# Transposed blocks of the attention probabilities: one store to DRAM and four loads for each four heads, in place of 16 copies from SBUF to SBUF

## The chip, the cores and the metric

The kernel runs on one core of a Trainium2 chip, in one launch. The metric is the device time in microseconds (us). Three runs of the kernel before gave 1243.25, 1243.53 and 1244.83 us; their median, 1243.53 us, is the time to compare with. The profile comes from an execution of its own, which took 1242.96 us.

## What is computed

The reference is one block of a transformer with a mixture of experts, all of it in float32: 16 sequences of 256 tokens with 256 channels, 16 heads of 64, and 8 experts with 1024 hidden channels. Cut to what matters here:

```python
shift = silu(t) @ W_ada.T + b_ada
h = ln(x) + shift
q, k, v = heads(h @ Wqkv.T)            # q and k are normalised per head
attn = softmax(q @ k.T / sqrt(64))     # 256 x 256 for each head and sequence
x = x + merge(attn @ v) @ Wout.T
tok = x.reshape(-1, 256)               # 4096 tokens
gate = softmax(tok @ Wgate.T)
vals, idx = top_k(gate.T, 512)         # each expert takes its best 512 tokens
tok[idx] += gelu(ln(tok[idx]) @ fc1.T + b1) @ fc2.T * vals
```

The product `attn @ v` sums over the keys, so TensorE wants the probabilities with the keys on the partitions, while the softmax leaves the queries there. The change is in how the probabilities are turned round.

## The kernel before, in words

**The stages.** For each sequence b (16 of them) the kernel normalises the tokens (`First`), projects them in twelve groups of 512 columns (`Group`: queries, keys and values for each half of the tokens), works through the attention in four steps of four heads (`Quad`, d = 0 to 3), and closes with the output projection, the residual and the gate logits for each of the two halves of the tokens (`Tail`). When the gates of the first 15 sequences are known, a search of 30 steps over the bits of the gate values (`Routing`) finds each expert's threshold. Each step is a comparison on VectorE, a count on TensorE (tile `pc`) and a decision on VectorE, and each needs the one before it. The experts (`Job`) follow, and the last sequence is routed beside them.

**One Quad.** `scores` puts the scores of two heads into PSUM (L612), `maxima` takes the row maxima on VectorE (L619), `exps` the exponentials on ScalarE (L628), `normalise` divides on GpSimd (L639). `turn` (L649) transposes on VectorE within blocks of 32 x 32, from `pr` into `pb`: it leaves each block on its own 32 partitions, so that the blocks still have to change partitions. `shuffle` (L661) does this: for each of four groups of 32 source partitions (k) and each of four groups of 32 target partitions (q) it issues one copy of 64 KB on SyncE's queue, from `pb` to `prT`, both in SBUF. `product` (L672) then multiplies `prT` by the values into `po` on TensorE, and `evict` (L683) copies `po` out on ScalarE. `pb` and `prT` have two buffers each, 8 KB in each partition, and `po` has one.

**The order.** Nothing runs in the order of the source. Every step is recorded with `at(place, engine, duration, function, needs, makes, tiles, lag)`; `Plan.order` plays all steps through with these durations, always takes on a free engine the ready step with the smallest place, and emits the instructions in the order that results. The tables `PLACES` (one list for the first, the second, the inner and the last two sequences) and `OTHERS` hold the places. So the durations and lags given there, and the tables, decide in which order each engine's queue holds its instructions; on the chip each engine works through its queue in order and waits at each instruction for what it needs. The steps in question, with the durations that the plan takes for them:

```python
at(p + 13, "SP", 6.8, a.shuffle, [pb], [prT], [pb, prT], lag=2.4)
at(p + 22 + i, "PE", 0.87, partial(a.product, i), [prT, ("v", b, g)], [po], [po, prT, ("v", b)], mode=2, lag=0.25)
```

SyncE's queue (SP) also carries the loads of the inputs `xs` (L396), the stores of the tokens `out` (L705) and of the normalised tokens `xn_dram` (L715), and, from the routing on, the loads of the experts' weights (L965 to L969). The instruction that waits there holds up all that stand behind it.

Of the kernel before, what the change touches and what calls it, by code (L numbers as in the profile page):

```python
# [9 lines left out]
F32 = mybir.dt.float32  # L10
# [8 lines left out]
P = 128  # L19
B, N, D = 16, 256, 256  # L20
# [6 lines left out]
TB = N // P  # L27
# [7 lines left out]
SQ = 32  # L35
QB = P // SQ
GW = 512
# [105 lines left out]
def kernel(  # L143
# [14 lines left out]
    nc = tc.nc  # L158
# [68 lines left out]
    def make_others():  # L227
# [32 lines left out]
            -1072.21, -115.42, -267.12, -318.46, -283.78, -263.97, -343.54, -141.99, -236.37,  # L260
            -14.78, -117.8, -186.09, -160.29, 25.3, -57.16, -43.18, -123.28, -79.21, -42.36,
            -113.65, 19.5, -72.88, -20, -70.8, -105.24, 11.94, -75.55, 182.09, -53.2, 2.24,
            -32.28, -39.46, 109.35, 45.26, -50.6, 154.41, -26.02, -58.37, -126.26, -142.08,
            210.89, -27.08, -38.07, -37.13, 5.73, 56.69, -23.35, -19.55, -25.71, -35.68, -18.12,
            74.55, 7.69, -21.8, 114.43, 8.66, -10.45, 70.24, 156.18, 1.21, 12.27, 1.88, 131.08,
            -15.51, 119.21, 116.23, -1.79, 79.85, -8.01, -63.9, -48.12, -63.85, -73.53, 47.46,
            -99.13, -127.82, -186.87, -153.57, 84.76, -127.47, -28.96, 127.88, -174.52, -111.4,
            -104.14, -19.09, -47.87, -8.05, 80.09, -63.95, 106.51, -63.42, -122.29, -8.5,
            171.03, -189.33, -37.82, 290.18, 281.18, -29.55, 19.38, 112, 128.87, -12.2, 186.07,
            91.29, 46.71, 173.2, 114.86, -9.77, 109.32, 149.87, -2.6, -9.22, 0.91, -13.41,  # L270
            134.45, 44.98, -24.62, -65.96, -17.99, -3.34, 260.18, -7.67, 17.8, 35.74, 230.8,
            -2.03, 167.88, 59.79, 281.61, 33.31, 279.56, 29.61, 22.41, 106.55, 15.76, 44.1,
            17.21, 11.13, 77.2, 165.28, 142.54, -60.91, -3.37, 69.59, 88, 16.75, 337.51, 91.2,
            34.07, 4.36, 19.11, 45.9, 31.58, 8.25, 114.95, 164.25, 23.63, 54.39, 128.79, 117.81,
            29.1, 147.8, 161.75, 207.73, 239.85, -42.55, 34.67, 125.98, 63.81, 65.48, 87.98,
            -22.22, 40.48, 79.92, 130.41, 49.27, 238.8, 60.37, 155.11, 191.23, 86.22, 164.95,
            161.39, 80.09, 90.21, 56.48, 51.85,
        ),
        1: (
            -1032.77, 129.62, -236.19, -178.16, -149.32, -47.96, -192.61, -79.27, 33.09, -10.98,  # L280
            -69.57, 52.12, -62.93, 196.91, -51.34, 58.21, 154.36, -36.67, -14.18, 55.12, -44.86,
            61.84, -27.82, -5.29, -36.21, 126.18, 82.92, -42.83, -28.04, 101.38, -11.56, -33.27,
            115.69, 59.37, -41.86, -34.28, 36.18, 48, -29.52, -1.38, 130.85, 23.18, -26.62,
            21.73, 23.95, -26.66, 22.46, -16.79, 104.79, -25.2, 16.34, 21.7, -17.15, -14.75,
            120.88, -18.87, 64.57, -12.33, -22.41, 12.98, -13.56, 129.3, 86.67, -10.79, -0.15,
            -14.51, 18.77, -4.63, 129.64, 13.06, -38.88, -1.19, 53.22, 95.23, 2.6, -15.23,
            55.21, 14.48, 121.02, -6.64, 96.51, 53.51, -5.52, 38.03, -5.28, 133.71, -4.22,
            291.78, 38.02, 1.66, 144.11, 3.99, 31.85, -2.69, 183, -82.98, -23.55, 44.17, 57.53,
            13.82, 7.93, 121.24, 28.25, 7.73, 230.34, 24.33, 57.51, 56.5, 185.27, 15.11, 155.8,
            8.4, 18.56, 19.91, 14, 69.92, 48.81, 184.98, -14.57, -46.18, 61.75, 40.25, 119,  # L290
            0.56, 294.7, 12.02, 16.1, 4.67, 93.62, 16.4, 231.42, 36.38, 76.89, 89.11, 17.69,
            119.85, 148.17, 157.6, 18.58, 64.15, 136.41, 119.23, 93.08, 1.87, 2.62, 24.02,
            181.34, 32.12, 294.16, 72.21, 85.72, 23.9, 318.14, 148.32, 111.52, 7.8, 159.92,
            81.55, 33.83, 42.79, 146.1, 106.8, 29.25, 189.76, 83.08, 261.31, 125.98, 19.94,
            222.2, 133.41, 47.61, 112.18, 196.94, 88.54, 185.36, 217.24, 77.64, 74.55, 155.64,
            63.8, 252.59, 208.61, 85.49, 155.93, 79.33, 114.81, 72.16, 81.95, 89.11,
        ),
        7: (
            -136.6, 28.37, -210.72, -195.86, 106.16, 217.69, -207.27, 16.33, -60.67, 77.55,
            -55.88, -39.27, -51.01, 63.44, -48.12, -45.3, -11.11, -53.32, -35.85, -45.42, 11.39,  # L300
            -42.14, -24.52, 104.14, -46.62, 127.86, -16.95, -39.73, -42.11, 44.56, -17.26,
            -44.54, 36.77, 24.84, -38.59, 83.06, -21.91, -43.85, 219.41, -45.58, 199.34, 56.38,
            -36.69, -22.93, 5.22, -11.48, -23, 64.04, -34.53, -36.25, 113.75, -22.27, 214.83,
            -17.15, -6.77, -16.98, -18.81, -18.51, 151.77, -14.04, -8.89, -3.49, 10.95, -14,
            32.32, -14.28, 20.86, -8.78, -0.9, 87.46, -11.05, -2.93, 5.15, -10.42, 52.71, -5.41,
            57.43, 12.4, 23.37, -11.7, 35.64, 43.51, 53.16, 136.74, 101.97, 69.01, -1.54,
            246.65, 13.35, 2.69, 125.8, 2.34, 17.7, 44.42, -8.16, -27.24, 35.18, 158.76, 154.51,
            6.05, 68.56, 90.55, 211.51, 6.57, 87.13, 145.2, 18.76, 60.22, 125.88, 11.56, 135.85,
            15.4, 132.04, 67.4, 12.06, 86.81, 113.28, 44.43, 112.93, -19.04, -6.2, 145.87,
            31.58, 15.43, 161.05, 94.62, 131.83, 14.43, 71.38, 119.46, 290, 39.56, 151.25,  # L310
            93.87, 19.72, 169.02, 127.15, 45.38, 20.48, 41.14, 61.17, 183.17, 80.13, -3.1,
            27.05, 17.75, 56.16, 20.46, 277.99, 206.07, 104.18, 22.24, 70.57, 154.95, 146.92,
            37.98, 34.46, 87.02, 31.68, 60.48, 90.07, 47.36, 26.9, 69.95, 217.97, 57.1, 299.85,
            12.13, 146.35, 63.74, 80.61, 163.92, 222.82, 99.04, 73.18, 334, 64.46, 129.48, 71.3,
            79.93, 277.53, 173.17, 111.17, 330.87, 101.91, 94.77, 82.32, 120.45, 87.81,
        ),
        14: (
            -148.14, -203, -234.48, -237.91, 55.19, 13.44, -208.2, 38.61, -85.25, 81.97, -56.75,
            -17.65, -54.82, -22.75, -43.34, 107.24, 56.31, -60.46, -60.46, -44.39, -5.57,
            -50.76, 57.85, -38.65, -34.07, -34.22, -28.53, 50.07, -28.8, 77.55, 65.27, -54.99,  # L320
            -24.28, -45.45, -41.95, 43.06, -39.78, 16.46, 82.74, -2.8, 243.5, 82.1, -30.81,
            58.24, -10.38, -27.02, -21.75, 54.73, 33.7, -29.06, -22.77, 185.55, 94.16, -22.99,
            237.62, -22.46, -28.6, -6.64, -6.52, -19.5, 47.39, -23.44, 189.71, -16.88, -12.68,
            24.5, 108.76, -14.16, -13.79, 22.95, -21.66, -27.51, 66.22, 100.67, -7.05, -23.3,
            -14.3, 94.87, -21.87, -12.56, 54.22, -22.99, 32.84, -3.13, 166.41, -12.6, -8.66,
            88.05, 83.14, -3.53, 87.02, -4.59, -11.23, 4.89, 61.68, -27.92, 65.35, 62.04, 83.34,
            2.36, 3.96, 173.51, 117.22, 5.12, -5.35, 59.99, 48.05, 74.16, 137.59, 200.97, 5.88,
            3.1, 109.29, 79.47, 7.14, 115.94, 9.24, 28.59, -1.22, -1.02, 64.19, 129.58, 136.77,
            12.87, 38.68, 215.83, 16.25, 16.68, 36.84, 15.14, 170.59, 89.28, 284.22, 95.61,
            16.71, 214.12, 191.35, 94.06, 26.68, 16.76, 202.03, 240.43, 145.78, 10.7, 11.64,  # L330
            45.82, 171.36, 30.75, 305.13, 43.03, 105.79, 28.98, 188.53, 165.45, 141.02, 27.29,
            47.93, 222.73, 34.77, 86.81, 131.92, 66.48, 31.53, 46.64, 55.06, 94.94, 292.48,
            12.99, 127.48, 63.84, 87.84, 48.33, 196.73, 81.43, 120, 476.87, 68.18, 57.54,
            141.33, 68.28, 126.03, 174.39, 148.26, 318.47, 55.44, 239.95, 72.76, 135.74, 72.97,
        ),
        15: (
            -96.34, 57.5, -135.71, -164.35, 65.69, -163.41, -140.57, 25.18, -76.44, -14.76,
            -67.45, 31.26, -64.27, 60.26, -64.64, -55.24, -7.71, -56.48, -52.05, -39.56, -59.56,
            10.57, -38.4, 101.96, -46.67, 127.7, -41.61, -47.88, -29.51, -0.69, -10.21, -51.73,
# [42 lines left out]
    if True:  # L382
# [216 lines left out]
        class Quad:  # L599
# [44 lines left out]
            def turn(self, i, j):  # L644


                if self.pb is None:
                    self.pb = work.tile([P, 2 * QB, 4, TB, SQ], F32, tag="pb", bufs=2, name="pb")
# [442 lines left out]
        at = plan.step  # L1091
# [276 lines left out]
```

## Time and profile before

| what | value |
|---|---|
| median of three runs | 1243.53 us |
| the profiled execution | 1242.96 us |
| its span on the core | 1241.2 us |
| TensorE matmuls busy | 1092.9 us, 88% |
| VectorE busy | 805.5 us, 65% |
| ScalarE busy | 591.2 us, 48% |
| GpSimd busy | 576.4 us, 46% |
| moved by DMA | 129.54 MB, 104 GB/s on the mean |
| of it read from HBM and written to it | 48.56 MB and 12.58 MB |
| `shuffle` copies | 1024 of 64 KB |

The span is what lies between the first and the last instruction of the core; 1.8 us of the execution lie outside it. In the profile, PE is TensorE's matmul side and PEld its weight loads; DVE is VectorE, ACT is ScalarE, POOL is GpSimd and SP is SyncE (SPq in the rows of its DMA issues). A row "out<-in" names the tile that an instruction writes and the tiles that it reads, without buffer numbers. "Idle before" is the time that an engine stood still ahead of the instructions of a row, followed by what ended the wait.

By the rows of SyncE, the stores of `xn_dram` that begin each later sequence's tail stand at 262.67 us and, eight sequences on, at 698.35 us. The attention stage runs from about 31 to 907 us, the search from 907.06 to 960.74 us, and the experts from 985.45 us to the end.

### The profile page before, as it was taken

How to read it: one execution, taken by the hardware profiler on the slowest of the kernel's cores; microseconds unless marked ns; L12 is line 12 of the kernel's file. 1: busy time of each engine (PE TensorE's matmuls, PEld its weight loads, DVE VectorE, ACT ScalarE, POOL GpSimd, SP SyncE). 2: the span in 40 equal slices, each digit the busy share in tenths (PEclk: the TensorE clock that was granted, in tenths of full speed). 3: DMA queues.
4: the chain of work that ended last, by engine and by line, in shares of the span. 5: the costliest groups of instructions: out<-in, count | busy, mean ns of one | idle time of the engine just before them, and what ended most of it. 6: DMA issues, size and time to landing. Idle time of an engine off the chain costs nothing. (4 is left out here: it accounts for less than half of the span.)

```text
span 1241.2 us, 18995 instructions
## 1 busy us (share of the span) xinstructions
PE 1092.9 (88%) x5787; PEld 721.4 (58%) x5787; DVE 805.5 (65%) x2364; ACT 591.2 (48%) x1661; POOL 576.4 (46%) x805
## 2 busy tenths in 40 slices
PE   6888899899999989999998999989933699999996
PEld 4444555465555646555564656546511588888886
DVE  6657566667776666776767677757656648855540
ACT  1556455556555556655546555555510333333331
POOL 2556445546555554565555455545430233333332
PEclk9899999999999999999999999999956799999999
DMA  5023233333334233332423333323521345656661
GB/s 188 1 68 81 73 91 96 93 92 93 95 81 108 78 102 97 94 99 69 113 74 101 93 92 85 105 73 102 151 76 35 107 146 171 192 162 187 190 187 33
DMA packets 128661, 129.54 MB, mean 104 GB/s; under 512 B 20272, under 2 KB 121904, under 8 KB 128560
## 3 DMA queue, kind: packets, MB, share of 16 engines
q1 hardware_dynamic: 118784, 116.20, 32.8%
q0 software_dynamic: 6144, 8.39, 3.6%
q10 hardware_dynamic: 3632, 3.74, 0.9%
q8 instruction: 47, 0.77, 0.3%
q14 instruction: 54, 0.44, 0.1%
HBM read 48.56 MB, written 12.58 MB: 49 GB/s over the span
## 5 line engine op out<-in xcount | busy, mean ns | idle before, releaser
L537 PE MATMUL pm<-wq,hT 128*128 128x512 f32 x768 | 357.6, 605 | 7.7 <-issue 4.9
L181 POOL TENSOR_TENSOR ss<-ss,neghalf 128x8 f32<-128x8 f32 x128 | 210.9, 1651 | 271.2 <-DVE ss L558 268.4
L639 POOL TENSOR_SCALAR pr<-pr,sums 128x256 f32<-128x256 f32 x512 | 235.9, 478 | 79.5 <-DVE sums L635 79.5
L628 ACT ACTIVATE pr<-sc,nmax 128x256 f32<-128x256 f32 x512 | 237.7, 479 | 30.7 <-DVE nmax L619 24.8
L537 PEld LDWEIGHTS pm<-wq,hT 128*128 128x128 f32 x768 | 139.1, 193 | 152.2 <-issue 138.8
L672 PE MATMUL po<-prT,v 128*64 128x256 f32 x1024 | 136.5, 406 | 84.8 <-DMA prT<-pb 71.6
L619 DVE TENSOR_REDUCE nmax<-sc 128x2 f32<-128x512 f32 x256 | 164.7, 674 | 53.9 <-PE sc L612 53.7
L649 DVE STREAM_TRANSPOSE pb<-pr 128x512 f32<-128x512 f32 x256 | 175.3, 698 | 31.8 <-POOL pr L639 18.5
L672 PEld LDWEIGHTS po<-prT,v 128*64 128x64 f32 x1024 | 78.9, 142 | 142.3 <-issue 79.3
L612 PE MATMUL sc<-kT,qT 64*128 64x256 f32 x1024 | 146.8, 407 | 0.8 <-DVE ss L558 0.6
L612 PEld LDWEIGHTS sc<-kT,qT 64*128 64x128 f32 x1024 | 90.8, 189 | 57.9 <-issue 46.1
L554 DVE TENSOR_REDUCE ss<-sq 128x8 f32<-128x512 f32 x128 | 86.5, 676 | 56.9 <-ACT sq L550 56.3
L683 ACT COPY oT<-po 128x512 f32<-128x512 f32 x64 | 37.5, 585 | 176.7 <-PE po L672 176.7
L1047 PE MATMUL ph<-xT,w 128*128 128x256 f32 x512 | 119.7, 388 | 0.1
L694 PE MATMUL pw<-wo,oT 128*128 128x256 f32 x512 | 116.7, 381 | 0.0
L1063 PE MATMUL py<-w,hid 128*128 128x256 f32 x512 | 116.3, 380 | 0.0
L570 DVE TENSOR_TENSOR qk<-pm,ss 128x512 f32<-128x512 f32 x128 | 86.5, 683 | 34.1 <-POOL ss L181 33.2
L628 ACT ACTIVATION_READ_ACCUMULATOR pr<-sc,nmax 128x1 f32 x512 | 108.3, 212 | 0.0
L694 PEld LDWEIGHTS pw<-wo,oT 128*128 128x128 f32 x512 | 96.2, 191 | 19.3 <-issue 7.0
L1080 POOL DMA_INDIRECT out<-y,idx x32 | 51.4, 1605 | 120.7 <-DVE y L1074 71.3
L1047 PEld LDWEIGHTS ph<-xT,w 128*128 128x128 f32 x512 | 96.9, 193 | 13.6 <-ACT xT L1035 0.2
L1063 PEld LDWEIGHTS py<-w,hid 128*128 128x128 f32 x512 | 95.6, 190 | 12.8
(133 smaller groups left out, 1078.6 us busy)
## 6 DMA issues: line engine op xcount, KB each, us to landing
prT<-pb SPq DMA_DIRECT2D x1024, 64.0 KB, 2.0
w<-in_fc2T SPq DMA_DIRECT2D x16, 1024.0 KB, 5.5
w<-in_fc1T SPq DMA_DIRECT2D x16, 1024.0 KB, 8.0
xn_dram<-tn SPq DMA_DIRECT2D x32, 128.0 KB, 1.8
out<-tok SPq DMA_DIRECT2D x32, 128.0 KB, 2.0
xs<-in_x SPq DMA_DIRECT2D x12, 256.0 KB, 3.0
b<-in_b2s SPq DMA_DIRECT2D x16, 128.0 KB, 8.1
wq<-in_wqkvT SPq DMA_DIRECT2D x3, 512.0 KB, 6.1
```

Source lines behind the costliest of these rows:

```text
L181: nc.gpsimd.tensor_tensor(dst, src, neghalf[:, : src.shape[1]], ALU.pow)
L537: nc.tensor.matmul(self.pm, hTs[self.b][:, c, bass.ts(self.t, P)], wq[:, c, bass.ts(self.g, GW)], start=(c == 0), stop=(c == DC - 1),)
L554: nc.vector.tensor_reduce(self.ss[:, 0, :], self.sq.rearrange("p (h d) -> p h d", d=HD), AX.X, ALU.add,)
L612: nc.tensor.matmul(self.sc[i, j][:, t, :], qTs[self.b][rows, hp, bass.ts(t, P)], kTs[self.b][rows, hp, :], start=True, stop=True,)
L619: nc.vector.tensor_reduce(self.nmax[i, j], self.sc[i, j], AX.X, ALU.max, negate=True)
L628: nc.scalar.activation(self.pr[i, j][:, t, :], self.sc[i, j][:, t, :], AF.Exp, bias=self.nmax[i, j][:, t : t + 1], scale=1.0, accum_out=se ...
L639: nc.gpsimd.tensor_scalar(self.pr[i, j][:, t, :], self.pr[i, j][:, t, :], self.sums[i][:, 1, j, t : t + 1], 1.0, ALU.mult, ALU.mult,)
L649: nc.vector.transpose(self.pb[:, :, 2 * i + j].rearrange("p k t n -> p t k n"), self.pr[i, j].rearrange("p t (k m) -> p t k m", m=SQ),)
L672: nc.tensor.matmul(self.po[j * HD : (j + 1) * HD, i, :], vs[self.b][:, c, bass.ts(4 * self.d + 2 * i + j, HD)], self.prT[:, c, :, 2 * i + ...
L694: nc.tensor.matmul(self.pw, oTs[self.b][:, hp // 2, self.t, hp % 2, :], wo[:, hp, :], start=(hp == 0), stop=(hp == HP - 1),)
L1047: nc.tensor.matmul(self.ph[f], self.w1[:, c, bass.ts(f, P)], self.xT[:, c, :], start=(c == 0), stop=(c == DC - 1),)
L1063: nc.tensor.matmul(self.py[i], self.hid[:, f, bass.ts(i, P)], self.w2[:, f, :], start=(f == 0), stop=(f == FC - 1),)
```

## The change

`turn` writes `pb` in another order of blocks, `shuffle` goes, and two steps take its place. `away` stores the whole of `pb` (1 MB, 8 KB from each of the 128 partitions) to a DRAM tile `blocks`, and `back` reads it in four loads of 256 KB, each into 32 partitions, in runs of 2 KB. `product` reads `prT` with its dimensions in the new order. `blocks` has two buffers. In the plan the one step on SP of 6.8 us with a lag of 2.4 becomes one of 0.4 us with a lag of 5.0 and one of 1.8 us with a lag of 4.0; the lag after each TensorE step goes from 0.25 to 0.22; and the tables `PLACES` and `OTHERS` hold other numbers throughout, so that the order on every engine is another one. The core of the diff:

```diff
                 if self.pb is None:
-                    self.pb = work.tile([P, 2 * QB, 4, TB, SQ], F32, tag="pb", bufs=2, name="pb")
+                    self.pb = work.tile([P, QB, TB, 4, TB, SQ], F32, tag="pb", bufs=2, name="pb")
                 nc.vector.transpose(
-                    self.pb[:, :, 2 * i + j].rearrange("p k t n -> p t k n"),
-                    self.pr[i, j].rearrange("p t (k m) -> p t k m", m=SQ),
-                )
-
-            def shuffle(self):
-                self.prT = work.tile([P, TB, QB, 4, TB * SQ], F32, tag="prT", bufs=2, name="prT")
-                src = self.pb.rearrange("p (c k) h t n -> p c k (h t n)", c=TB)
-                for k in range(QB):
-                    for q in range(QB):
-                        nc.sync.dma_start(
-                            self.prT[bass.ts(q, SQ), :, k].rearrange("p c h n -> p c (h n)"),
-                            src[bass.ts(k, SQ), :, q],
-                        )
+                    self.pb[:, :, :, 2 * i + j].rearrange("p k c t n -> p t c k n"),
+                    self.pr[i, j].rearrange("p t (c k m) -> p t c k m", c=TB, m=SQ),
+                )
+
+            def away(self):
+                self.blocks = dram.tile([QB, SQ, QB, GW], F32, tag="blocks", bufs=2, name="blocks")
+                nc.sync.dma_start(
+                    self.blocks.rearrange("k m q n -> (k m) (q n)"),
+                    self.pb.rearrange("p q c h t n -> p (q c h t n)"),
+                )
+
+            def back(self):
+                self.prT = work.tile([P, QB, TB, 4, TB * SQ], F32, tag="prT", bufs=2, name="prT")
+                for q in range(QB):
+                    nc.sync.dma_start(
+                        self.prT[bass.ts(q, SQ)].rearrange("p k c h n -> p k (c h n)"),
+                        self.blocks[:, :, q].rearrange("k m n -> m k n"),
+                    )
...
-                            self.prT[:, c, :, 2 * i + j, :],
+                            self.prT[:, :, c, 2 * i + j, :],
...
-            sums=4, pr=5, pb=2, prT=2, tok=3, tn=2, tokT=2, pa=1, l1=4, l2=4,
+            sums=4, pr=5, pb=2, prT=2, blocks=2, tok=3, tn=2, tokT=2, pa=1, l1=4, l2=4,
...
-                    at(p + 22 + i, "PE", 0.87, partial(a.product, i), [prT, ("v", b, g)], [po], [po, prT, ("v", b)], mode=2, lag=0.25)
-                at(p + 13, "SP", 6.8, a.shuffle, [pb], [prT], [pb, prT], lag=2.4)
+                    at(p + 22 + i, "PE", 0.87, partial(a.product, i), [prT, ("v", b, g)], [po], [po, prT, ("v", b)], mode=2, lag=0.22)
+                blocks = ("blocks",) + n
+                at(p + 13, "SP", 0.4, a.away, [pb], [blocks], [pb, blocks], lag=5.0)
+                at(p + 18, "SP", 1.8, a.back, [blocks], [prT], [blocks, prT], lag=4.0)
```

## The prediction

> **What bounds the kernel now.** First the page: busy shares and slices.
>
> ```profile
> PE 1092.9 (88%) x5787; PEld 721.4 (58%) x5787; DVE 805.5 (65%) x2364; ACT 591.2 (48%) x1661; POOL 576.4 (46%) x805
> ...
> PE   6888899899999989999998999989933699999996
> ...
> PEclk9899999999999999999999999999956799999999
> DMA  5023233333334233332423333323521345656661
> ```
>
> TensorE is nearly full in the attention (slices 2 to 28) and in the experts (the last ten); between them lies the search, with PE at 3. The DMA engines are a third busy in the attention, so they don't bind by bandwidth. Next, the groups and the list of waits, for what ends TensorE's idle time:
>
> ```profile
> L672 PE MATMUL po<-prT,v 128*64 128x256 f32 x1024 | 136.5, 406 | 84.8 <-DMA prT<-pb 71.6
> ...
> L649 DVE STREAM_TRANSPOSE pb<-pr 128x512 f32<-128x512 f32 x256 | 175.3, 698 | 31.8 <-POOL pr L639 18.5
> ```
> ```profile
> PE po L672 <- DMA prT<-pb: 71.6, 41, 10.5
> PE pc L868 <- DVE reach L859: 22.8, 26, 1.1
> PE pls L1003 <- DVE gates L737: 8.3, 1, 8.3
> PE pm L537 <- issue: 4.9, 1, 4.9
> ```
>
> Ahead of `product` TensorE stood still for 84.8 us, mostly for the copies of `shuffle`; hardly anything else in the attention holds it. By stage, the idle time put before L672 (waits list with windows, all releasers) is 20.9 us up to 262 us, 32.7 in the eight sequences from 262 to 698, 16.0 from 698 to 908 and 15.4 in the search. Last, one of these waits in order of time, on SP's queue and on PE:
>
> ```profile
> 534.01 10.19 SPq L661 DMA_DIRECT2D prT<-pb  x16
> 544.30 0.53 SPq L396 DMA_DIRECT2D xs<-in_x  x1
> ```
> ```profile
> 543.23 1.88 PE L537 MATMUL pm<-wq,hT 128*128 128x512 f32 x4
> 546.12 1.95 PE L672 MATMUL po<-prT,v 128*64 128x256 f32 x16 [1.01 <-DMA prT<-pb]
> ```
>
> The 16 copies take 10.19 us to issue (0.64 each), the last lands 2.0 us after its issue, and `product` starts 12.1 us after the first. The bound is not bandwidth but one queue's rate of issue. The plan reckoned with 6.8 + 2.4 = 9.2 us, so it placed `product` some 3 us too early. Four times a sequence that makes 32.7 / 8 = 4.1 us; the period is (698.35 - 262.67) / 8 = 54.5 us, so TensorE has 50.4 us of work in each.
>
> **What the change costs, part by part.** Durations come from these DMA rows:
>
> ```profile
> prT<-pb SPq DMA_DIRECT2D x1024, 64.0 KB, 2.0
> w<-in_fc2T SPq DMA_DIRECT2D x16, 1024.0 KB, 5.5
> w<-in_fc1T SPq DMA_DIRECT2D x16, 1024.0 KB, 8.0
> xn_dram<-tn SPq DMA_DIRECT2D x32, 128.0 KB, 1.8
> out<-tok SPq DMA_DIRECT2D x32, 128.0 KB, 2.0
> xs<-in_x SPq DMA_DIRECT2D x12, 256.0 KB, 3.0
> ```
>
> *Removed:* 16 issues x 0.64 = 10.2 us of SP for each Quad.
>
> *The store (`away`).* No row shows 1 MB stored. It lies between the 128 KB stores (1.8 us) and `fc1T`, 1 MB queued behind another (8.0); I take 5.5, the row of its size. With 0.1 us for the wait ahead, 5.6.
>
> *The loads (`back`).* Four issues, 0.64 apart as now, the last landing like the 256 KB load `xs`: 3 x 0.64 + 3.0 = 4.9 us; with 0.3 for the two semaphores, 5.2. Below, 3 x 0.64 + 2.0 = 3.9; above, `fc1T`'s 8.0. Together 10.8 us, against 12.1: a chain only 1.3 us shorter, by SP's issue time (5 x 0.64 = 3.2 against 10.2) and not by latency.
>
> *The wait added.* `back` waits on SP for the store's landing. In the built program's order the inner sequences stand so on SP: away A, away B, back A, store `out`, back B, store `xn`, away C, store, load `xs`, store, away D, back C, back D. Behind a waiting `back` stand `away` of the next Quad or stores that nobody needs soon. Only `back` C is held by another Quad: it stands behind `away` D, which the order places 3.6 us of TensorE's work ahead of the end of A's product, for which `back` C waits anyway.
>
> *The new order.* This decides. Counting TensorE's work between the instructions in the built order (L537 x4 1.75 us, L612 x8 1.06, L672 x16 1.88, L579 x4 0.45, starts of successive rows of the timeline): before, 9 to 9.5 us stand between `shuffle` and `product`. After, A and B are loaded some 23 us ahead of their products; no wait. C and D take the `prT` buffers of A and B, so their loads start when those products end. From the end of A's product to C's stand two scores, B's product, one transposition and one projection: 2.1 + 1.9 + 0.45 + 1.75 = 6.2 us; from B's to D's, 6.6. Against 5.2 us both are covered, by 1.0 and 1.4. I leave 0.5 us per period: 4 of the 32.7 us; gain **28.5**.
>
> *Start to 262 us.* Here one Quad follows the next. The work between the first DMA and `product` rises from 8.7 us (first eight Quads) to 9.6 (first seven), and the chain is 1.3 shorter: 2.2 us, about what a wait is now (18.9 us in 9). The largest (5.5) is partly left: 9 of 20.9 us; gain **12**.
>
> *698 to 907 us.* The distances from store to product are 10.4 to 36 us; 3 of 16.0 us remain; gain **13**. Besides, 3.5 us of projection stand before the search now and inside it afterwards; gain **3.5** here.
>
> *The search.* It takes 53.7 us, while its 30 steps come every 1.01 us (949.62 to 959.74 us holds ten), 30.4 us. The rest is the last three products: PE's queue waits 10.5 and 4.4 us for their copies with the counts behind. After, both stores stand after step 3 and the two products at steps 13 and 15. Two projections, two products and one output projection stand between the steps, 3.5 + 3.8 + 3.5 = 10.8 us, of which each of five hides 0.84 us (the wait before a count): 6.6; VectorE's own work (two turns, a residual with its normalisation) 3 us. The second store lands behind the first (8.4 us), its loads 4.9 later: 13.3, against ten steps and a projection, 11; wait 2.3. Sum with 1.6 ahead of the first step: 30.4 + 6.6 + 3 + 2.3 + 1.6 = 43.9; gain **10**.
>
> *Nothing:* `turn` keeps its blocks and size (0.70 us; the 128x512 operations on VectorE lie between 0.67 and 0.70 whatever their pattern), `product` its runs of 64. VectorE is busy 38 to 39 of 55 us; if `turn` took twice as long, 16 x 0.7 = 11 us, it would be at 50 beside TensorE's 50.4.
>
> *What is late next.* With `product` on time, waits for VectorE and ScalarE (`nmax`, `qk`, `qT`) that it hid come into sight: on 13 periods 0.8 us each, **-10**.
>
> Sum: 28.5 + 12 + 13 + 3.5 + 10 - 10 = 57; 1242.96 - 57 = 1186. The profiled execution lies 0.6 us under the median, within the three runs.
>
> **A rule that speaks against it.** The copies' packets took 32.8% of 16 engines' span for 118784 packets of 1 KB, 54.8 ns each: 16 engines would move 1 MB in 3.7 us, under the 4.9 that I use. The Trainium skill (SBUF — State Buffer, Door 1: The DMA port swizzle) says that 32 partitions reach only 8 of the 16 ports, 189 GB/s measured for 1 MB and 218 at most. By that, an estimate, 1 MB of loads moves in 4.8 to 5.5 us, and with the 2 us before it C and D would wait 2.3 to 3.7 us per period. No row here shows large transfers into 32 partitions.
>
> **The rivals.**
> *A second wait for the loads (18%).* Let 1 MB into 32 partitions at a time move in y us. C lands 2 + y after its start, D behind it at 2 + 2y, and with 0.3 for semaphores both together wait 2y - 7.3 per period, since D's product stands 9.6 us after C's start. For: C and D load back to back, between other traffic. Against: the packets' 3.7 us. With y = 4.8 (halfway between 3.7 and 6.0, where `fc1T` lands at 8.0) 2.3 us, 1.8 more than I left, on 13 periods 23: **1209**; to 1230.
> *Another engine takes the wait's place (11%).* For: VectorE would be at 38.6 of 51 us. Against: its idle rows are waits for PE. At 2.5 us per period in place of 0.8, **1208**.
> *The change brings nothing (3%).* If the order, not the copies, made the waits: **1243**. Against: DMA ends 71.6 of 84.8 us.
> *Slower (6%).* The same loads, when they saturate: the gain of 57 us is gone when 13 periods wait 4.4 us more, 4.9 in all, y = 6.1 us; beyond that it is slower. With the longest landing of `fc1T`, 9.6 us (its line's instructions; the least is 5.6), y = 7.6, wait 7.9: 1186 + 13 x 7.4 = **1282**.
>
> **How the numbers follow.** The forecast has 62% (1168 to 1203: waits of 0 to 1.8 us per period). The range takes it and most of the first two rivals: 1168 to 1228, leaving the last two and their like. Faster by over 0.2% (about what a measurement of this kernel can tell from no change): the forecast and the first two rivals, 0.91; within it 0.03; slower 0.06.
>
> **What would show it.** `product`'s idle time falls from 84.8 to some 20 us; the period from 54.5 to 51 us; the search lasts 42 to 46 us; `blocks` lands in 5 to 6 us, `prT` in about 3; SP issues five DMAs for a Quad in about 3.2 us; HBM traffic rises by 134 MB. It is wrong if `prT` lands later than 4 us after the last issue, or if `nmax`, `qk` or `pb` end long waits of PE.

## The result, and the profile after

| | kernel before | changed kernel |
|---|---|---|
| median, measured side by side | 1243.39 us (1241.83 to 1244.83, 4 runs) | 1187.17 us (1186.60 to 1190.74, 4 runs) |
| ratio, 95% interval | 1 | 0.9554 (0.9532 to 0.9577) |
| profiled execution, span | 1242.96, 1241.2 us | 1186.62, 1184.9 us |

The forecast of 1186 us is met, 4.5% faster. The trace shows, though, that several of its terms were wrong and cancelled each other. Busy shares and slices of the changed kernel, from the page:

```profile
PE 1089.6 (92%) x5787; PEld 715.9 (60%) x5787; DVE 800.6 (68%) x2364; ACT 593.9 (50%) x1661; POOL 574.8 (49%) x805
...
PE   7899999999999999999999999999845799999996
...
PEclk8998999999999999999999999999966899999998
DMA  5147356656664647746665664746850366666661
```

TensorE has the same work (1090 us) in a shorter span. The DMA engines are twice as busy in the attention (mostly 4 to 7 tenths, before 2 to 4), since every transposed block now goes to DRAM and back. The groups of the two neighbours of the transfer, and the list of TensorE's waits, in total, number and longest:

```profile
L651 DVE STREAM_TRANSPOSE pb<-pr 128x512 f32<-128x512 f32 x256 | 171.7, 690 | 17.1 <-POOL pr L641 16.5
L679 PE MATMUL po<-prT,v 128*64 128x256 f32 x1024 | 135.0, 401 | 38.3 <-DMA prT<-blocks 34.5
```
```profile
PE po L679 <- DMA prT<-blocks: 34.5, 24, 5.2
PE pc L875 <- DVE reach L866: 19.7, 22, 2.2
PE pq L581 <- DVE qk L572: 6.4, 9, 2.1
```

`product` (L679) still stands still for 38.3 us, 84.8 before, and what ends this is still the transfer. No other engine has taken its place: the next waits are the counts of the search and `qk`, which is late nine times in the first sequences. `turn` (L651) costs what it did (690 ns, 698 before). The DMA rows, with the median time from issue to landing:

```profile
blocks<-pb SPq DMA_DIRECT2D x64, 1024.0 KB, 4.3
prT<-blocks SPq DMA_DIRECT2D x256, 256.0 KB, 6.5
...
out<-tok SPq DMA_DIRECT2D x32, 128.0 KB, 5.0
xn_dram<-tn SPq DMA_DIRECT2D x32, 128.0 KB, 4.1
```

The store is quicker than reckoned (5.5), the loads are much slower: 6.5 us where `xs` of the same size takes 3.0. One inner sequence in order of time shows the effect: SP's loads for two Quads (C and D, eight DMAs in one row of the first fence), and the products of C and of D on PE in the second.

```profile
422.74 4.67 SPq L668 DMA_DIRECT2D prT<-blocks  x8
```
```profile
430.42 1.95 PE L679 MATMUL po<-prT,v 128*64 128x256 f32 x16 [1.42 <-DMA prT<-blocks]
...
434.95 1.08 PE L679 MATMUL po<-prT,v 128*64 128x256 f32 x8 [0.93 <-DMA prT<-blocks]
```

C's product starts 7.7 us after its first load was issued and D's 12.2 us after it, each late by about a microsecond; A's and B's products never wait here. From 262 to 698 us these waits sum up to 19.1 us in eight sequences, 2.4 us in each.

To see where the time went, both traces are cut at nearly the same work: the first output projection of sequence 3 and of sequence 11, the first instruction of the search (`pgT`) and its end (the sums `po<-tot`), and the first matmul of the experts.

| stage | before, us | after, us | gain | forecast |
|---|---|---|---|---|
| start to sequence 3 | 307.7 | 286.9 | 20.8 | 12 |
| eight inner sequences | 436.3 | 420.5 | 15.8 | 28.5 |
| to the search | 163.2 | 146.2 | 16.9 | 13 + 3.5 |
| late next, over all the attention | | | (within the above) | -10 |
| search | 53.7 | 54.5 | -0.8 | 10 |
| search to experts | 24.7 | 22.2 | 2.5 | 0 |
| experts to the end | 255.8 | 254.7 | 1.1 | 0 |
| sum | 1241.2 | 1184.9 | 56.3 | 57 |

Nearly the whole gain is made in the attention: 53.5 us, where 47 was forecast. The search brings none of its 10.

### The profile page after: what moved, and what is told of

Read it like the earlier page. It is cut to its first block, busy times and chain, and to the rows that moved or that the text cites. A ratio compares the mean times of both kernels' runs of the same rounds, so it can differ in the third digit from the quotient of the medians.

```text
span 1184.9 us, 17925 instructions
## 1 busy us (share of the span) xinstructions
PE 1089.6 (92%) x5787; PEld 715.9 (60%) x5787; DVE 800.6 (68%) x2364; ACT 593.9 (50%) x1661; POOL 574.8 (49%) x805
## 5 line engine op out<-in xcount | busy, mean ns | idle before, releaser
L539 PE MATMUL pm<-wq,hT 128*128 128x512 f32 x768 | 363.8, 610 | 5.5 <-DVE wq L461 3.5
L651 DVE STREAM_TRANSPOSE pb<-pr 128x512 f32<-128x512 f32 x256 | 171.7, 690 | 17.1 <-POOL pr L641 16.5
L679 PE MATMUL po<-prT,v 128*64 128x256 f32 x1024 | 135.0, 401 | 38.3 <-DMA prT<-blocks 34.5
L614 PE MATMUL sc<-kT,qT 64*128 64x256 f32 x1024 | 142.2, 400 | 0.1
L679 PEld LDWEIGHTS po<-prT,v 128*64 128x64 f32 x1024 | 73.0, 141 | 105.8 <-issue 33.9
L701 PE MATMUL pw<-wo,oT 128*128 128x256 f32 x512 | 120.6, 391 | 0.0
L701 PEld LDWEIGHTS pw<-wo,oT 128*128 128x128 f32 x512 | 99.2, 196 | 25.6 <-issue 9.4
L552 ACT ACTIVATE sq<-pm 128x512 f32<-128x512 f32 x128 | 76.7, 600 | 74.4 <-PE pm L539 70.3
L1070 PEld LDWEIGHTS py<-w,hid 128*128 128x128 f32 x512 | 95.5, 190 | 12.7
```

Source lines behind the costliest of these rows:

```text
L539: nc.tensor.matmul(self.pm, hTs[self.b][:, c, bass.ts(self.t, P)], wq[:, c, bass.ts(self.g, GW)], start=(c == 0), stop=(c == DC - 1),)
L614: nc.tensor.matmul(self.sc[i, j][:, t, :], qTs[self.b][rows, hp, bass.ts(t, P)], kTs[self.b][rows, hp, :], start=True, stop=True,)
L651: nc.vector.transpose(self.pb[:, :, :, 2 * i + j].rearrange("p k c t n -> p t c k n"), self.pr[i, j].rearrange("p t (c k m) -> p t c k m", ...
L679: nc.tensor.matmul(self.po[j * HD : (j + 1) * HD, i, :], vs[self.b][:, c, bass.ts(4 * self.d + 2 * i + j, HD)], self.prT[:, :, c, 2 * i + ...
L701: nc.tensor.matmul(self.pw, oTs[self.b][:, hp // 2, self.t, hp % 2, :], wo[:, hp, :], start=(hp == 0), stop=(hp == HP - 1),)
L1070: nc.tensor.matmul(self.py[i], self.hid[:, f, bass.ts(i, P)], self.w2[:, f, :], start=(f == 0), stop=(f == FC - 1),)
```

## The experiments

**The theories.** Mine: 16 issues on SP were the bound, the DRAM path takes them away, the new order makes use of it, and what is left of the waits is the slow loading of 32 partitions at a time. Rivals: the new order alone brings the gain; the path alone does; the waits that are left are another engine's; the search is held by something else than its transfers.

**1. The new order with the old copies.** `away` issues nothing, `back` issues the 16 copies; the order on every engine stays that of the changed kernel.

```diff
             def away(self):
-                self.blocks = dram.tile(...)
-                nc.sync.dma_start(self.blocks..., self.pb...)
+                pass
             def back(self):
-                for q in range(QB):
-                    nc.sync.dma_start(self.prT[bass.ts(q, SQ)]..., self.blocks[:, :, q]...)
+                for k in range(QB):
+                    for q in range(QB):
+                        nc.sync.dma_start(self.prT[bass.ts(q, SQ), k]..., self.pb[bass.ts(k, SQ), q]...)
```

> The new kernel with its order kept, but the store left out and the four loads replaced by the 16 copies from SBUF to SBUF. Theory (SyncE's issue time makes the chain, and the order only uses what the chain leaves): C's copies start when A's product ends and take 10.2 us to issue and 2.3 more, 6.3 us beyond the 6.2 us of TensorE's work ahead of its product; D's follow behind them on the queue. Together some 13 us of waits per inner sequence against 2.3 now: about 1320 us. Rival (the new order alone brings the gain, the path does not matter): 1185 to 1205 us.

Measured: 1362.38 us, ratio 1.0932 (1.0878 to 1.0987). The order alone makes the kernel 9% slower, so the rival falls. It is slower still than expected, and by another road. The waits of VectorE, and those of TensorE:

```profile
DVE pb L651 <- DMA prT<-pb: 221.1, 36, 15.1
```
```profile
PE pq L581 <- DVE qk L572: 118.0, 21, 13.0
PE po L675 <- DMA prT<-pb: 20.7, 10, 7.6
```

And those of SP's queue, ahead of the copies (L664):

```profile
SPq L664 <- DVE pb L651: 120.1, 15, 14.4
SPq L664 <- PE po L675: 112.1, 14, 11.0
```

I had expected `product` to wait for late copies; it waits 20.7 us. It is `turn` that stands 221.1 us, until the copies have read `pb`, and behind it in VectorE's queue stands `qk`, for which TensorE waits 118.0 us. The copies go from `pb` straight into `prT`, so they need a free `prT`: for 112.1 us SP waits for a product (L675) that frees one. In this order C and D take the buffers of A and B, and `pb` stays full until then. The store needs no `prT`, and in the changed kernel no wait of `turn` for a DMA is left. So the DRAM tile is also one more buffer between `turn` and `product`, a part of the change that the prediction did not see. (How the 9% divides between this and the 10 us of issue, this run does not tell.)

**2. The DRAM path in the old order.** The kernel before, with the store and the four loads in the place of the 16 copies (`pb` and `prT` laid out as in the changed kernel; only the core is shown):

```diff
+            def shuffle(self):
+                self.away()
+                self.back()
```

> The kernel before with its order kept, with the store and the four loads at the place of the 16 copies. Theory (a chain shorter by 1.5 us takes as much off each of some 41 waits of 1.7 us, more in the search): about 1205 us, the waits for prT down from 72 us to 25 to 35. Rival (the order decides, the chain is as long as before since the loads land 6.5 us after their issue): 1235 to 1245 us.

Measured: 1212.85 us, ratio 0.9711 (0.9671 to 0.9752). The path alone brings 2.9%, the path with the new order 4.5%: of some 55 us (0.0446 x 1243) about 36 (0.0289 x 1243) come with the path in the old order and 20 with the order on top of it. Waits of `product` for the loads in this kernel:

```profile
PE po L681 <- DMA prT<-blocks: 53.7, 33, 9.6
```

They were expected to fall to 25 to 35 us. In this profile, of the slowest of the four runs (1219.85 us), `product` stands still for 58.7 us in all, 84.8 before. The old order places `product` too early for this chain as well; neither half of the change does the whole.

**3. Four stores of 32 partitions, one load of 128.** The change of partitions is done by the store instead of the load; order and bytes are the same.

```diff
-                nc.sync.dma_start(self.blocks.rearrange("k m q n -> (k m) (q n)"), self.pb...)
+                for k in range(QB):
+                    nc.sync.dma_start(self.blocks[:, :, k].rearrange("q m n -> m q n"), self.pb[bass.ts(k, SQ)]...)
...
-                for q in range(QB):
-                    nc.sync.dma_start(self.prT[bass.ts(q, SQ)]..., self.blocks[:, :, q]...)
+                nc.sync.dma_start(self.prT..., self.blocks.rearrange("q m k n -> (q m) (k n)"))
```

> The new kernel with the split on the other side of DRAM: four stores, each from 32 partitions, and one load of 1 MB into all 128 partitions. Theory (loads into 32 partitions move at about 200 GB/s, which makes the waits of C and D): the load lands in about 4.5 us, under the 6.2 us of cover, the waits of 2.3 us per inner sequence go, and the longer stores are hidden by their distance: 1157 us, down to 1150 if the search gains too. Rival (the loads are slow because of the traffic beside them): 1180 to 1192 us.

Measured: 1159.59 us, ratio 0.9294 (0.9250 to 0.9339), some 28 us faster than the changed kernel by the medians (32 by the ratios). Its group of `product`:

```profile
L679 PE MATMUL po<-prT,v 128*64 128x256 f32 x1024 | 131.9, 394 | 15.3 <-DMA prT<-blocks 14.0
```

The waits for the loads fall from 34.5 to 14.0 us, and from 262 to 700 us a single one is left (1.6 us), with no wait of another engine in its place. Alone, the four stores take 6.1 us and the one load 4.9 (experiment 4), so the chain is hardly shorter than 3.9 + 7.5; only the half that C and D wait for is. So the 2.4 us of each inner sequence were the four loads, and nothing that VectorE or ScalarE would have imposed anyway. Up to the search TensorE stands 21 us less than in the changed kernel and is also 7.5 us less busy (799.9 against 807.4) with the same instructions; what makes them shorter was not looked into. The search is as long as before: 54.3 us.

**4. The transfers by themselves.** This kernel computes nothing of the result; it issues each transfer alone, with a VectorE copy behind it that waits for the landing.

```diff
+        nc.sync.dma_start(kmqn..., src...)                       # the store
+        for q in range(QB):                                       # the four loads
+            nc.sync.dma_start(dst[bass.ts(q, SQ)], kmqn[:, :, q].rearrange("k m n -> m k n"))
+        nc.sync.dma_start(dst..., qmkn.rearrange("q m k n -> (q m) (k n)"))   # one load, 128 partitions
```

> Computes none of the reference's result; it only writes zeros to the output and then makes each transfer by itself, each group after the one before has landed. If 32 partitions limit the rate: four loads of 256 KB into 32 partitions each end about 7 us after the first issue, one load of 1 MB into 128 partitions 4.5 us, eight loads 12 us, four stores from 32 partitions 6.5 to 7 us against 4.3 for one store. If it is the traffic beside them: four loads end after 4.5 to 5 us like the one, eight after 7.5 to 8. The 16 copies: 11.5 to 12 us in both.

The timeline of the four loads, and of the one load (SP's issue, and the VectorE copy that waits for it):

```profile
105.39 1.97 SPq L100 DMA_DIRECT2D dst<-kmqn  x4
112.91 0.15 DVE L81 COPY dst<-dst 128x1 f32<-128x1 f32 x1 [7.55 <-DMA dst<-kmqn]
...
120.46 0.34 SPq L105 DMA_DIRECT2D dst<-qmkn  x1
125.38 0.15 DVE L81 COPY dst<-dst 128x1 f32<-128x1 f32 x1 [4.95 <-DMA dst<-qmkn]
```

| transfer | from first issue to last landing, to 0.2 us |
|---|---|
| store of 1 MB from 128 partitions | 3.9 us |
| four stores of 256 KB, each from 32 partitions | 6.1 us |
| one load of 256 KB into 32 partitions | 3.6 us |
| four such loads, 1 MB | 7.5 us |
| four in the order 0, 2, 1, 3 | 7.2 us |
| four with each partition's 8 KB in one run | 7.0 us |
| eight loads, 2 MB | 12.3 us |
| one load of 1 MB into 128 partitions | 4.9 us |
| 16 copies in SBUF | 10.1 us of issue, 2.0 to land |

A load of 256 KB alone was well sized (3.6, by `xs` 3.0). But loads into 32 partitions do not overlap: each further one adds (7.5 - 3.6) / 3 = 1.3 us, not the 0.64 us of an issue, and four more add 12.3 - 7.5 = 4.8 us for 1 MB, 218 GB/s. With 3.6 - 1.3 = 2.3 us of fixed latency, an estimate, the load into 128 partitions moves its 1 MB in 2.6 us, some 400 GB/s. Longer runs change little (7.0), and so does another order (7.2). That four DMAs are slow because they are four, whatever their partitions, was not tried, but two rows speak against it: a 256 KB load into 128 partitions (`xs`) takes 3.0 us against 3.6, and of the experts' weights, two loads of 1 MB into 128 partitions issued 0.42 us apart, the second lands 3.1 us behind the first in the changed kernel (median of 16), not 4.8. So the partitions decide, as far as these rows show.

**5. A higher clock in the search.** The clock granted in the search of the changed kernel is 0.69 on the mean, and some rows of matmuls there take nearly twice as long (the output projection 6.48 us, 3.62 elsewhere). Here TensorE gets four transpositions, whose output nobody reads, behind each count.

```diff
                 nc.tensor.matmul(self.pc, ...)
+                if n:
+                    fill(4)
```

> The new kernel with four transposes of the identity, whose result nobody reads, behind each count of the search but the last, in the 0.84 us for which TensorE waits there. Theory (the search gained nothing because work that the order moved into it runs at a granted clock of 0.69: 6.3 us for an output projection that takes 3.6 elsewhere, 3.6 for a projection of 1.75): the clock in the search rises to 0.9 or more, the projection takes 3.6 to 4 us, and the search falls from 54.5 to 47 to 49 us; the whole 1180 to 1182 us. Rival (the clock doesn't answer to such short work, or the fills delay the counts as much as they save): 1186 to 1192 us.

Measured: 1185.78 us, ratio 0.9509 (0.9481 to 0.9538), which just overlaps that of the changed kernel (0.9532 to 0.9577). First what the search of the changed kernel looks like on PE, then the same instructions here:

```profile
871.78 3.76 PE L539 MATMUL pm<-wq,hT 128*128 128x512 f32 x4
...
880.74 1.97 PE L679 MATMUL po<-prT,v 128*64 128x256 f32 x8 [5.20 <-DMA prT<-blocks]
...
895.41 6.48 PE L701 MATMUL pw<-wo,oT 128*128 128x256 f32 x16
```
```profile
876.45 1.88 PE L539 MATMUL pm<-wq,hT 128*128 128x512 f32 x4
...
884.59 1.97 PE L679 MATMUL po<-prT,v 128*64 128x256 f32 x8 [5.75 <-DMA prT<-blocks]
...
900.75 3.62 PE L701 MATMUL pw<-wo,oT 128*128 128x256 f32 x16
```

The clock rises to 0.88 and the output projection falls from 6.48 to 3.62 us, but the search only from 54.5 to 52.9 us, not to the 47 to 49 expected: what is saved before the product returns as wait there. From the first instruction of the search to this product it is 27.2 us in the changed kernel (880.74 - 853.58) and 27.0 us here (884.59 - 857.59).

**6. Split stores and filled counts together.** Experiments 3 and 5 in one kernel.

> The four stores and the one load together with the filled search. If the two effects lie in different stages they add up: 1152 to 1154 us, against 1159.6 with the loads alone. If the fills bring nothing: 1157 to 1163 us.

Measured: 1157.92 us, ratio 0.9298 (0.9273 to 0.9323), the same as experiment 3. The search takes 52.9 us there. A higher clock alone changes little; the first half of the search holds it.

**7 and 8. The products of the search later.** In the plan alone, the last two Quads of the last sequence get a longer lag for `back`. The only effect on any engine's order is that their products stand behind counts 19 and 21 of the search, not 13 and 15: six more counts can run while the loads land. Experiment 7 does it to kernel 6, experiment 8 to the changed kernel.

```diff
-                at(p + 18, "SP", 1.8, a.back, [blocks], [prT], [blocks, prT], lag=4.0)
+                at(p + 18, "SP", 1.8, a.back, [blocks], [prT], [blocks, prT], lag=13.0 if b == B - 1 and d > 1 else 4.0)
```

> The kernel with four stores, one load and filled counts, with one thing more: in the search the products of the last two Quads stand six counts later (behind counts 19 and 21, not 13 and 15). Every other instruction on every engine has its place. Theory (the search's first half is held by the store and load of the last two Quads, and counts that could run in that time stand behind the product that waits): the wait of 5.4 to 5.8 us before the first of these products goes, the search falls from 53 to 47 or 48 us, and the whole to 1151 to 1154 us. Rival (the counts themselves, a chain of VectorE and TensorE, bound the search, so that the wait only changes its place): 1157 to 1159 us, no difference.

> The changed kernel (one store, four loads, counts not filled) with the same six counts ahead of the products of the last two Quads, and nothing else moved. Theory: the wait of 5.2 us in the search goes; 1181 to 1183 us against 1187. Rival (the counts run at a low clock, and six more of them in a row take as long as the wait): 1186 to 1188 us.

(Kernels 5 to 8 ran on another chip than 1 to 4; ratios, each to runs of the kernel before on the same chip, are what compares across.) Measured: experiment 7 gave 1151.33 us, ratio 0.9249 (0.9218 to 0.9281), all its four runs (1149.72 to 1155.23) under all of kernel 6 (1157.23 to 1159.34); experiment 8 gave 1178.61 us, ratio 0.9468 (0.9441 to 0.9494), clear of the changed kernel's interval and below the 1181 to 1183 expected. The first of the moved products and the output projection in 8, and the first product in 7:

```profile
878.81 1.98 PE L679 MATMUL po<-prT,v 128*64 128x256 f32 x8
...
887.67 3.70 PE L701 MATMUL pw<-wo,oT 128*128 128x256 f32 x16
```
```profile
856.26 1.08 PE L679 MATMUL po<-prT,v 128*64 128x256 f32 x8
```

The bracket with the wait is gone in both. The search lasts 47.4 us in 8 (850.11 to 897.55; 54.5 in the changed kernel) and 45.5 us in 7 (829.03 to 874.57; 52.9 in kernel 6). Both theories' rivals, that the counts bind anyway, fall. But in 8 the wait is not all: of the 7.1 us that the search gains, the products with their wait bring 4.9, read as below from the row of counts, and the output projection brings 2.8, since it follows the products more closely here and runs at a granted clock of 1.00 (0.56 in the changed kernel), with no count filled; smaller rows take back 0.6. (Another 3.5 us between these two profiles lie ahead of the search, where the order is the same: that is spread between runs.) In 7 against 6 the projection takes 3.62 us in both, and the search gains 7.3 us. Kernel 7 is the fastest here, 7.5% under the kernel before.

## Why the prediction was right, and where only its sum was

That the sum came out within 1 us is luck. The bound was read rightly and the change does lift it, but the inner sequences gained 12.7 us less than forecast and the search 10.8 less, while the term of -10 did not come, the start gained 8.8 more and the time behind the search 3.6 that nobody reckoned.

**The bound** was read rightly. SP's 10.2 us of issue for each Quad go, and `product` waits 38.3 us in place of 84.8 (some 20 were expected); experiments 1 and 2 show that it is the path that frees the order.

Of the signs named, HBM traffic rose by 134 MB as said (61.1 to 195.4), SP issues a Quad's five DMAs in 2.1 to 2.7 us (3.2), and the period is 52.6 us (51).

**The store** was taken at 5.5 us; it lands in 4.3 (3.9 alone). It is not what C and D wait for: in experiment 3 the stores take longer (6.1 alone), and their waits go.

**The loads are the step that failed: "Four issues, 0.64 apart as now, the last landing like the 256 KB load `xs`: 3 x 0.64 + 3.0 = 4.9 us".** Four loads take 7.5 us, because 1 MB into 32 partitions at a time moves in 4.8. `xs` goes to 128 partitions, and a row of the right size but on the wrong number of partitions was taken. By the forecast's own sign (`prT` landing later than 4 us after the last issue) this step was wrong: in the fence of 422.74 us C's product waits until 7.7 us after the first load's issue, and four issues take only some 2.3. The chain from store to product is 3.9 + 7.5 = 11.4 us alone, hardly under the 12.1 of the copies. In the old order, where most products wait for their chain, that little counts many times: over the 64 Quads of experiment 2 the median from the last `turn` to the product is 12.5 us, 13.2 in the kernel before, and the 36 us of experiment 2 come without the chain lying anywhere else. (64 x 0.7 = 45 us, an estimate, is enough for them; that this is all of them is not shown.) What the new order adds is that the chain can lie elsewhere: from the store's issue to the product the changed kernel has a median of 28.1 us, the kernel before 12.1 from the first copy. Two of the four Quads are loaded well ahead, and C and D wait.

**C and D covered, 0.5 us of wait per period**: it was 2.4. The first rival had the mechanism and the formula: 2y - 7.3 gives 2.3 us at y = 4.8, and 4.8 is what experiment 4 measured. So the inner sequences gained 15.8 us instead of 28.5. The forecast gave this rival 18%, and held the packets' 3.7 us against it, a figure from copies spread over all the partitions. The Trainium skill (SBUF — State Buffer, Door 1: The DMA port swizzle) had it right: 32 partitions reach half of the ports, 218 GB/s at most. The four further loads' 218 GB/s agree, beside some 400 for 128 partitions; the ports themselves no run here shows. The page was weighed and put second.

**"What is late next", -10**: it did not come. In the inner sequences one wait of 1.4 us for another engine is left, and in experiment 3 none; 8 of the 13 periods of that term are the inner ones. This error has the opposite sign, and with the start (20.8 for 12) it hid the first. Of the start's 20.8 us some 13 are waits for the transfer (21.5 before, 8.1 after), as forecast; the rest is the new order's own start, which was not traced further.

**698 us to the search**: 16.9 for 16.5, right.

**The search, gain 10**: it lost 0.8. The forecast's 43.9 us missed four things, read from the PE timeline as the time that each adds to the row of counts. The lead-in has another product ahead of step 1, which waits 2.24 us and runs 3.4: 6.0 us in place of 1.6. The two projections cost 3.5 us in place of 1.8, and the output projection 5.3 in place of 2.7, since some of these matmuls run at a low clock (0.56 granted during the output projection). The wait and the products cost 7.8 in place of 4.4: from the first of the two stores to the product it is 17.7 us (863.09 to 880.74) where 8.4 + 4.9 = 13.3 were reckoned, for the eight loads alone take 12.3. VectorE's work was 1.7 us less than assumed. 43.9 + 4.4 + 1.7 + 2.7 + 3.4 - 1.7 = 54.4. Experiment 5 shows that of these the clock by itself is worth 1.6 us while the wait stands, experiment 8 that the wait with the products is worth 4.9, and that without it the output projection is 2.8 us shorter too. The forecast let counts hide work that stands in the queue, but an engine works in order: the counts behind the waiting product could hide nothing. It had seen this in the kernel before ("PE's queue waits ... with the counts behind") and did not carry it over.

**After the search**, 3.6 us that nobody reckoned: the output projection that was moved into the search was done behind it before.

**The rivals that fell**: "another engine takes the wait's place" (no such wait in the inner sequences of experiment 3), "nothing", and "slower", whose point of y = 6.1 us was not reached at 4.8. Experiment 1 shows how near another road to slower lay: the same order with `pb` held longer.

## What to carry to other kernels

Size a DMA by a row with the same number of partitions, not only the same bytes, and put the side that touches few partitions where the chain has slack: with the four 32-partition stores early and one wide load late, the same bytes in the same order were worth another 28 us. An intermediate tile in DRAM is also a buffer; ask what it lets go of earlier before putting its whole gain down to issue time. And when a transfer must be covered by a serial loop on an in-order engine, move the instruction that waits behind the steps that are to cover it: six counts ahead of it took 7 us off the search, some 5 of them the wait itself, and a faster clock alone took off less than 2.

## What the runs showed of the hardware

- Loads into 32 partitions issued back to back add 1.1 to 1.3 us per 256 KB, whether 2 KB or 8 KB lie together; into 128 partitions 1 MB lands in 4.9 us.
- The time to issue a DMA on SP does not follow its bytes: 0.34 us for the store of 1 MB, 0.43 (median) for a load of 256 KB, 0.64 for each copy of 64 KB between partitions.
- Small stores land later beside large transfers on the same queue: the 128 KB of `out` and `xn_dram` take 5.0 and 4.1 us, 2.0 and 1.8 before. No wait of TensorE or VectorE for them stands in the changed kernel's lists.
- In the search, a loop of short matmuls that wait for one another, the clock granted to TensorE falls: 0.74, 0.70 and 0.62 in three stretches, and a row of 16 matmuls takes 6.48 us in place of 3.62. Four idle transpositions behind each count bring it back to 3.62, for 116 matmuls more, and the counts still come 1.0 to 1.1 us apart. An order with three counts between the last product and this row, not nine, does nearly the same without them (experiment 8: 3.70 us).
